# State-space input projections from seven quarter products, in four portions per chunk, with decays in place and five row buffers at the start

## Chip, core and metric

One core of one Trainium2 chip runs the whole program in one launch. The time is that of one execution on the device, in microseconds (us); a kernel's time is the median of several runs. The engines are named as in the profile: PE (TensorE) for matmuls, PEld for its weight loads, DVE (VectorE), ACT (ScalarE), POOL (GpSimd), and SP, whose queue issues most DMAs.

## Reference

All in float32, on 1024 tokens of width 512. Six steps are added to x one after another, each on the layer norm of x:

```
x = x + 0.5 * expert_ffn(norm(x))      # 8 experts, top 2, relu
x = x + attention(norm(x))             # 32 heads of 128, causal
x = x + 0.5 * expert_ffn(norm(x))
x = x + 0.5 * lora_ffn(norm(x))        # 512 x 512, plus a rank-8 expert of 4
x = x + state_space(norm(x))
x = x + 0.5 * lora_ffn(norm(x))
```

The change is mostly in the state-space step, with 64 heads of 64 channels in 8 groups and a state of 128:

```
proj = h @ in_proj_w.T                  # gate 4096 | x 4096, B 8x128, C 8x128 | dt 64
xBC  = silu(conv_bias + sum_k pad(x,B,C)[:, k:k+L] * conv_weight[:, k])    # 4 taps
dt   = softplus(dt + dt_bias);  dA = exp(dt * A)
state_t = state_{t-1} * dA_t + (dt_t * x_t) B_t ;  y_t = state_t . C_t + D * x_t
yn   = y * rsqrt(mean over the group of y^2 + eps) * norm_weight * silu(gate)
out  = yn @ out_proj_w.T
```

## The kernel before

The tokens are eight tiles of 128 (`NT`), x stays in SBUF in float32, and `hT` holds the normalized rows transposed: 128 partitions by four k-blocks (`KT`) by 1024 tokens. A list-scheduling layer (tiles with pools) takes the program order, places instructions on each engine's in-order queue, moves independent ones past each other, and adds the semaphore waits that tiles in use need. So the order on an engine is close to the text, but not equal to it.

**The start.** `expert_ffn` loads all expert weights, and `before_rows` runs `gate_steps` over the eight tiles: `normalize` writes the row `ln_xn` (pool `lnp`, two buffers, L169) and stores it to DRAM through ACT's queue (L172); then come the transposes into `hT` and the gate's logits. After the routing, rows are gathered back by indirect DMA on POOL's queue.

**Attention** already forms its projections from seven products of quarters: `sums` (L621) makes sums of weight quarters on POOL (L632), `products` (L246) the seven products, `mm_qk` (L821) and `mm_v` (L794) issue the matmuls, the latter with 256 columns (L797).

**State space** (`mamba`, L905). A first pipeline of tiles finishes the second expert step, runs the lora step, and computes dt, its decays and their running products; `decay` in DRAM holds the decays and their cumulative products in a form that can be broadcast to all partitions. Then come the units: `units` lists 8 groups times 2 halves of the tokens. A unit has four chunks of 128 tokens. While the scan of one unit runs, the projections of the next are interleaved:

- `project_pair(un, j)` (L1092): j = 0 for B and C, 1 and 2 for x, 3 and 4 for the gate. It fills one PSUM tile `ps_in` of 128 x 1024 (pool `pbig`, two buffers) by `project` (L227): two outputs, each four matmuls of 512 columns. A float32 matmul is two records in the profile. `plan` puts j = 0 and 1 beside chunk 0, then one pair beside each of chunks 1, 2 and 3.
- `conv_silu` (L1053): ACT writes the current tap with the bias (L1055), DVE adds three taps (L1059), reading `ps_in` in PSUM; in the second half, three more short steps take the last three columns of the first half from `hist` (L1068), which the first half keeps (L1077); ACT applies silu (L1078). D x is one ACT step per 128 channels over the half (`xd`, L1122).
- `finish_bc` (L1129): transposes of B and the products of B and C, masked into `gt`.
- `prepare(un, i)` (L1151): loads a chunk's decays twice over (`dd`, L1157, SP's queue), makes the segment decays `e_seg` by a DVE scan (L1163) and a product with `gt` (L1171), `xdt` = dt x from transposes (L1176), `xw` on POOL (L1182) and `cs` on POOL (L1188).
- `scan(un, i)` (L1196): `ps_y` (L1206), `y_m` (L1215), its squares (L1219) that POOL folds (L1238, L1239), `yg` (L1221), and the state: `ps_st` (L1224), POOL's decay of the state (L1231) and DVE's addition (L1234).
- `project_out` (L1243): the sum of squares `ps_ss` (L1247), its power on DVE and POOL (L149, L150), the output `ps_out` (L1258) and its addition to x (L1261).

`load_group(g)` issues the four weight loads of a group (`w_bc`, `w_x`, `w_g`, `w_out`) before its first projection; `wpool` has four buffers, so each waits for the last reader of the same weights of the group before. The loop's body is:

```
done = scan(un, i, *ready)
for j in plan[i]:
    project_pair(nxt, j)
if i == 1: finish_bc(nxt)
ready = prepare(un, i + 1)        # or prepare(nxt, 0)
project_out(*done)
```

Of the kernel before, what the change touches and what calls it, by code (L numbers as in the profile page):

```python
# [75 lines left out]
def macaron_kernel(  # L76
# [82 lines left out]
    def normalize(t, keep=False, pin=False):  # L159

        st = lnp.tile([P, 6], F32, tag="st", name="ln_st")
        nc.vector.bn_stats(st, x[:, t, :])
        mv = lnp.tile([P, 2], F32, tag="mv", name="ln_mv")
        nc.vector.bn_aggr(mv, st)
        rs = lnp.tile([P, 1], F32, tag="rs", name="ln_rs")
        root = rsqrt(rs, mv[:, 1:2], 1.0, EPS, 1)
        if pin:
            tc.keep_in_program_order(root)
        xn = lnp.tile([P, D], F32, tag="xn", name="ln_xn")  # L169
        nc.vector.tensor_scalar(xn, x[:, t, :], mv[:, 0:1], rs, ALU.subtract, ALU.mult)  # L170
        if keep:
            nc.scalar.dma_start(rows[t * P : (t + 1) * P, :], xn)  # L172
        normal[t] = xn
# [108 lines left out]
    def gates(t):  # L282
# [3 lines left out]
    gate_steps = (  # L286
        lambda t: normalize(t, True),
        transpose_h,
        None,
        lambda t: narrow_by_columns(t, gate_w, NE),  # L290
        gates,
    )
# [328 lines left out]
    def sums(pool, a11, a12, a21, a22, name, later=None):  # L621

        n = a11.shape[-1]
        ss = pool.tile([P, 3, 2, n], F32, tag=name, name=name)
        s1, s2, s4 = (ss[:, i, :, :] for i in range(3))
# [239 lines left out]
    class Scan:  # L865


        def __init__(self, pool):
# [9 lines left out]
            self.av = tile([P, MH], "av")  # L878

# [25 lines left out]
    def mamba(lora, par):  # L905
        conv, dsk, nwt, w_dt, dtb, av = par.conv, par.dsk, par.nwt, par.w_dt, par.dtb, par.av
        nct = MI // P
        with ExitStack() as ms:
# [10 lines left out]

            bcp = ms.enter_context(tc.tile_pool(name="m_bc", bufs=2))  # L920
            bp = ms.enter_context(tc.tile_pool(name="m_b", bufs=1))
            with tc.tile_pool(name="m_dt", bufs=1) as dp, tc.tile_pool(
# [5 lines left out]
                def pair():  # L928
                    return pairp.tile([P, 2, D], F32, tag="pair", name="pair")

# [70 lines left out]
                def add_bias(t):  # L1001
# [4 lines left out]
                    if t % nh == nh - 1:  # L1006
                        steps_of_time(t // nh)
# [15 lines left out]
            w2 = ms.enter_context(tc.tile_pool(name="m_w2", bufs=2))  # L1023
            ep = ms.enter_context(tc.tile_pool(name="m_e", bufs=2))
# [5 lines left out]
            def load_group(g):  # L1030

                gr = {"g": g, "state": None}
# [7 lines left out]
                gr["w_x"] = weights(in_wt[:, MI + g * 512 : MI + (g + 1) * 512], "w_x")  # L1040
                gr["w_g"] = weights(in_wt[:, g * 512 : (g + 1) * 512], "w_g")
# [8 lines left out]
                gr["hist"] = bcp.tile([P, 6, 3], F32, tag="hist", name="hist")  # L1050
                return gr

            def conv_silu(ps, ct, dst, hist, first):  # L1053

                nc.scalar.activation(  # L1055
                    dst, ps, AF.Identity, bias=conv[:, ct, 4:5], scale=conv[:, ct, 3:4]
                )
                for s in (1, 2, 3):
                    nc.vector.scalar_tensor_tensor(  # L1059
                        dst[:, s:],  # L1060
                        ps[:, : half - s],
                        conv[:, ct, 3 - s : 4 - s],
                        dst[:, s:],
# [3 lines left out]
                    if not first:  # L1067
                        nc.vector.scalar_tensor_tensor(  # L1068
                            dst[:, :s],
                            hist[:, 3 - s :],  # L1070
                            conv[:, ct, 3 - s : 4 - s],
                            dst[:, :s],
                            ALU.mult,
                            ALU.add,
                        )
                if first:
                    nc.vector.tensor_copy(hist, ps[:, half - 3 :])  # L1077
                nc.scalar.activation(dst, dst, AF.Silu)  # L1078

            def begin_unit(gr, hf):  # L1080
# [7 lines left out]
                un["xd"] = bcp.tile([P, 4, half], F32, tag="xd", name="xd")  # L1088
# [3 lines left out]
            def project_pair(un, j):  # L1092

                gr, g, hf = un["gr"], un["g"], un["hf"]
                ps = pbig.tile([P, S], F32, tag="pb", name="ps_in")
                w, col = ((gr["w_bc"], 0), (gr["w_x"], 0), (gr["w_x"], 256),
                          (gr["w_g"], 0), (gr["w_g"], 256))[j]
                for i in range(2):
                    project(ps, i * half, w, col + i * P, half, hf * half)
                if j > 2:  # L1100
                    i = 2 * (j - 3)
                    nc.scalar.activation(
                        un["sg"][:, i : i + 2, :].rearrange("p i c -> p (i c)"), ps, AF.Silu
                    )
                    return
                for i in range(2):
                    if j == 0:
                        dst = (un["bT"], un["cT"])[i]
                        ct = nct + i * MG + g
                    else:  # L1110
                        dst = un["xc"][:, 2 * (j - 1) + i, :]
                        ct = 4 * g + 2 * (j - 1) + i
                    conv_silu(
                        ps[:, i * half : (i + 1) * half],
                        ct,
                        dst,
                        gr["hist"][:, 2 * j + i, :],
                        hf == 0,
                    )
                    if j > 0:  # L1120
                        k = 2 * (j - 1) + i
                        nc.scalar.activation(  # L1122
                            un["xd"][:, k, :],
                            un["xc"][:, k, :],
                            AF.Copy,
                            scale=dsk[:, 4 * g + k : 4 * g + k + 1],
                        )
# [23 lines left out]
            def prepare(un, i):  # L1151
# [3 lines left out]
                dd = ep.tile([P, 2, HPG * P], F32, tag="dd", name="dd")  # L1155
                for q in range(2):
                    nc.sync.dma_start(  # L1157
                        dd[:, q, :],
# [3 lines left out]
                e = ep.tile([P, HPG, P], F32, tag="e", name="e_seg")  # L1162
                nc.vector.tensor_tensor_scan(  # L1163
                    e.rearrange("p h l -> p (h l)"),
                    dd[:, 0, :],
# [9 lines left out]
                xdt = w2.tile([P, D], F32, tag="xdt", name="xdt")  # L1175
                nc.vector.tensor_tensor(  # L1176
                    as_heads(xdt), as_heads(ps), per_head(dtp, un, i), ALU.mult
                )
                xw = None
                if c < NCH - 1:  # L1180
                    xw = w2.tile([P, D], F32, tag="xw", name="xw")
# [4 lines left out]
                if c > 0:  # L1186
                    cs = ep.tile([P, HPG, P], F32, tag="cs", name="cs")
# [3 lines left out]
                        dd[:, 1, :].rearrange("p (h l) -> p h l", l=P),  # L1191
                        ALU.mult,
                    )
                return e, xdt, xw, cs

            def scan(un, i, e, xdt, xw, cs):  # L1196
# [6 lines left out]
                for n, (left, right) in enumerate(terms):  # L1203
# [10 lines left out]
                y = w2.tile([P, 4, P], F32, tag="y", name="y_m")  # L1214
                nc.vector.tensor_tensor(  # L1215
                    y, py.rearrange("p (k l) -> p k l", l=P), un["xd"][:, :, tok], ALU.add
                )
                sq = w2.tile([P, 4, P], F32, tag="sq", name="sq")
                nc.scalar.activation(sq, y, AF.Square)  # L1219
                yg = w2.tile([P, 4, P], F32, tag="yg", name="yg")  # L1220
# [46 lines left out]
            gr = load_group(0)  # L1267
            un = begin_unit(gr, 0)
            for j in range(5):
                project_pair(un, j)  # L1270
                if j == 1:
                    finish_bc(un)
            ready = prepare(un, 0)
            plan = ((0, 1), (2,), (3,), (4,))
            for n, _ in enumerate(units):
                nxt = None
                if n + 1 < len(units):
                    g, hf = units[n + 1]
                    if hf == 0:
                        gr = load_group(g)  # L1280
                    nxt = begin_unit(gr, hf)
                for i in range(4):
                    done = scan(un, i, *ready)
                    if nxt is not None:
                        for j in plan[i]:
# [85 lines left out]
```

## Time and profile before

| | |
|---|---|
| median of 3 runs | 3006.68 us (3005.69 to 3007.23) |
| profiled execution | 3000.76 us, span 2999.0 us |
| mean granted clock of PE | 0.982 |
| busy PE, PEld | 2834.1 us (94%), 1525.5 us (51%) |
| busy DVE, ACT, POOL | 1691.8 us (56%), 711.6 us (24%), 782.8 us (26%) |
| DMA | 196.94 MB, mean 66 GB/s |

Busy time is the union of an engine's instructions; their records overlap a little at the ends, by some 0.08 us on DVE, so spacing is shorter than duration. The span can be cut into stages: the first expert step up to about 150 us, attention up to about 1640, the second expert step up to about 1800, the lora step and the decays up to about 1900, then the units up to about 2930. The shares of the whole span mix these stages, so each part of the change is read in its own. A line in a row is the line of the kernel before; "idle before" is the time for which the engine stood just before that group, with what ended it.

### The profile page before, as it was taken

How to read it: one execution, taken by the hardware profiler on the slowest of the kernel's cores; microseconds unless marked ns; L12 is line 12 of the kernel's file. 1: busy time of each engine (PE TensorE's matmuls, PEld its weight loads, DVE VectorE, ACT ScalarE, POOL GpSimd, SP SyncE). 2: the span in 40 equal slices, each digit the busy share in tenths (PEclk: the TensorE clock that was granted, in tenths of full speed). 3: DMA queues.
4: the chain of work that ended last, by engine and by line, in shares of the span. 5: the costliest groups of instructions: out<-in, count | busy, mean ns of one | idle time of the engine just before them, and what ended most of it. 6: DMA issues, size and time to landing. Idle time of an engine off the chain costs nothing.

```text
span 2999.0 us, 29327 instructions
## 1 busy us (share of the span) xinstructions
PE 2834.1 (94%) x10715; PEld 1525.5 (51%) x10715; DVE 1691.8 (56%) x3183; ACT 711.6 (24%) x1381; POOL 782.8 (26%) x593
## 2 busy tenths in 40 slices
PE   5979999999999999999999797899999999999989
PEld 3435646456464565645655343455555555555554
DVE  3145546465453654546545315677776777767673
ACT  1212212122121221213212121522222232322220
POOL 3231002020020200202000123144545545555450
PEclk8989999999999999999999898999999999999999
DMA  8420001010010100101002542232232322323210
GB/s 284 127 74 29 14 15 31 12 43 15 15 43 1 43 15 14 43 5 38 15 15 64 187 122 57 84 99 78 99 105 84 120 78 99 103 85 108 99 43 29
DMA packets 102174, 196.94 MB, mean 66 GB/s; under 512 B 9040, under 2 KB 34800, under 8 KB 102032
## 3 DMA queue, kind: packets, MB, share of 16 engines
q1 hardware_dynamic: 84896, 157.15, 15.7%
q0 software_dynamic: 6240, 20.45, 2.8%
q10 hardware_dynamic: 10896, 17.47, 1.5%
q8 instruction: 87, 1.43, 0.2%
q14 instruction: 55, 0.45, 0.1%
HBM read 176.17 MB, written 18.87 MB: 65 GB/s over the span
## 4 chain that ended last, share of the span: by engine, by line
PE 78%; DVE 12%; POOL 4%; issue 3%; DMA 2%; ACT 0%; POOLq 0%; DVEq 0%; SPq 0%; ACTq 0%
PE ps_in L227 14%; PE ps_m L823 13%; PE ps_o L728 8%; PE ps_wo L763 7%; PE ps_tr L156 6%; PE ps_m L797 6%; PE ps_out L1258 6%; PE ps_e L506 5%; PE ps_s L704 4%; DVE nm L715 3%; PE ps_y L1206 3%; PE ps_up L238 2%; DVE pr L720 1%; PE ps_st L1224 1%; DVE xc L1059 1%
## 5 line engine op out<-in xcount | busy, mean ns | idle before, releaser
L704 PE MATMUL ps_s<-kT,qT 128*128 128x512 f32 (+3 forms) x768 | 293.1, 491 | 1.8
L749 ACT COPY pT<-ps_tr 128x256 f32<-128x256 f32 (+2 forms) x192 | 91.9, 479 | 820.0 <-PE ps_tr L156 817.5
L728 PE MATMUL ps_o<-pT,v 128*128 128x512 f32 (+3 forms) x768 | 259.4, 488 | 0.0
L1258 PE MATMUL ps_out<-w_out,yg 128*128 128x512 f32 x512 | 240.4, 614 | 3.1 <-DVE yg L1221 3.1
L227 PE MATMUL ps_in<-hT,w_g 128*128 128x512 f32 x512 | 227.1, 596 | 7.9 <-issue 7.9
L227 PE MATMUL ps_in<-hT,w_x 128*128 128x512 f32 x512 | 225.8, 593 | 0.0
L1188 POOL TENSOR_TENSOR cs<-cT,dd 128x1024 f32<-128x1024 f32 x56 | 182.3, 3255 | 162.6 <-PE ps_y L1206 138.8
L763 PE MATMUL ps_wo<-w_o,oT 128*128 128x512 f32 x512 | 222.1, 593 | 0.0
L718 ACT ACTIVATE pr<-ps_s,nm 128x128 f32<-128x128 f32 (+7 forms) x256 | 190.3, 743 | 132.4 <-DVE nm L715 107.7
L728 PEld LDWEIGHTS ps_o<-pT,v 128*128 128x128 f32 x768 | 146.2, 191 | 142.6 <-issue 106.1
L156 PE MATMUL ps_tr<-ident,pr 128*128 128x128 f32 x1152 | 173.0, 277 | 31.1 <-DVE sm L719 22.9
L632 POOL TENSOR_TENSOR sv<-w_v 128x512 f32<-128x512 f32 x7 | 8.9, 1270 | 724.1 <-DMA w_v<-in_wkv_dram 607.3
L156 PEld LDWEIGHTS ps_tr<-ident,pr 128*128 128x128 f32 x1152 | 134.6, 142 | 115.1 <-issue 51.8
L715 DVE TENSOR_REDUCE nm<-ps_s 128x1 f32<-128x128 f32 (+7 forms) x256 | 189.2, 750 | 2.2
L506 PE MATMUL ps_e<-w_all,xt_s 128*128 (+1 forms) x368 | 167.0, 598 | 0.0
L227 PEld LDWEIGHTS ps_in<-hT,w_g 128*128 128x128 f32 x512 | 96.8, 191 | 127.5 <-issue 127.5
L227 PEld LDWEIGHTS ps_in<-hT,w_x 128*128 128x128 f32 x512 | 97.1, 190 | 120.8 <-issue 120.5
L1163 DVE TENSOR_TENSOR_SCAN e_seg<-dd,eye 128x1024 f32<-128x1024 f32 x64 | 154.2, 2409 | 6.9 <-PE ps_y L1206 5.7
L704 PEld LDWEIGHTS ps_s<-kT,qT 128*128 128x128 f32 x768 | 128.1, 193 | 54.7 <-issue 33.7
L763 PEld LDWEIGHTS ps_wo<-w_o,oT 128*128 128x128 f32 x512 | 96.4, 190 | 115.6 <-issue 115.6
L1059 DVE SCALAR_TENSOR_TENSOR xc<-ps_in,conv,xc 128x511 f32<-128x511 f32 (+2 forms) x192 | 141.6, 737 | 18.0 <-ACT xc L1055 17.6
L720 DVE TENSOR_SCALAR pr<-pr,sm 128x128 f32<-128x128 f32 (+7 forms) x256 | 145.4, 568 | 4.5
(252 smaller groups left out, 4401.8 us busy)
## 6 DMA issues: line engine op xcount, KB each, us to landing
dd<-decay SPq DMA_DIRECT2D x128, 512.0 KB, 4.5
w_all<-in_w_e_dram SPq DMA_DIRECT2D x16, 1024.0 KB, 10.3
outs<-y_e ACTq DMA_DIRECT2D x46, 256.0 KB, 3.6
w_v<-in_wkv_dram SPq DMA_DIRECT2D x8, 1024.0 KB, 5.2
w_q<-in_wq_dram SPq DMA_DIRECT2D x32, 256.0 KB, 4.3
w_k<-in_wkv_dram SPq DMA_DIRECT2D x8, 1024.0 KB, 5.2
w_o<-in_wo_dram SPq DMA_DIRECT2D x8, 1024.0 KB, 5.1
w_x<-in_in_wt_dram SPq DMA_DIRECT2D x8, 1024.0 KB, 7.8
```

The source lines that it names most:

```text
L156: nc.tensor.transpose(ps[:, i * P : (i + 1) * P], src(i), ident)
L227: nc.tensor.matmul(ps[:, cols : cols + n], lhsT=w[:, k, c0 : c0 + P], rhs=hT[:, k, t0 : t0 + n], start=(k == 0), stop=(k == KT - 1),)
L506: nc.tensor.matmul(ps, lhsT=xt[:, k, :], rhs=w_all[:, bass.ds(ep, 1), k, :].rearrange("p e c -> p (e c)"), start=(k == 0), stop=(k == KT - 1),
L704: nc.tensor.matmul(ps[:, j : j + m], lhsT=qT[:, qt * P : (qt + 1) * P], rhs=kT[:, j : j + m], start=True, stop=True,)
L715: nc.vector.tensor_reduce(nm, ps[:, :n], AX.X, ALU.max, negate=True)
L718: nc.scalar.activation(pr[:, :n], ps[:, :n], AF.Exp, bias=nm, accum_out=sm)
L728: nc.tensor.matmul(ps[:, lo:512], lhsT=v[:, kb, hh * P : (hh + 1) * P], rhs=pT[:, kb, lo:512], start=(kb == 0), stop=(kb == last),)
L763: nc.tensor.matmul(ps, lhsT=heads[hh][:, t * P : (t + 1) * P], rhs=w[:, hh, :], start=(hh == 0), stop=(hh == HG - 1),)
L797: nc.tensor.matmul(ps[:, t * 256 : (t + 1) * 256], lhsT=right[i][:, k, (j + t) * P : (j + t + 1) * P], rhs=left_v[i][:, k, :], start=(firs ...
L823: nc.tensor.matmul(ps, lhsT=gr["left"][i][:, k, hh * P : (hh + 1) * P], rhs=right[i][:, k, :], start=(first and k == 0), stop=(last and k ...
L1188: nc.gpsimd.tensor_tensor(cs, un["cT"][:, tok].unsqueeze(1).to_broadcast([P, HPG, P]), dd[:, 1, :].rearrange("p (h l) -> p h l", l=P), ALU ...
L1258: nc.tensor.matmul(po, lhsT=yg[:, k, :], rhs=w_o[:, k, :], start=(k == 0), stop=(k == 3))
```

## The change

**Seven products.** For each half, `quarter` makes the sums of the four quarters of `hT` once (on DVE, two k-blocks by 256 tokens each), one of them in place. `sums` makes those of the weights for B and C together, for x and for the gate, on POOL, into fixed tiles or into the free half of `w_bc`. A pair is now seven products of two matmuls with 256 columns in one PSUM tile: `pa` in one bank, `pb` and `pc` in the other. Three snapshots of `pa` go to SBUF by ACT, DVE adds them to `pb` and `pc`.

**Four portions.** `project_pair` is a generator; its four portions are placed before the scan, after it, after `prepare` and after `project_out`. The results of x, B and C go to `raw` tiles in SBUF with three columns ahead of them (zeros or `hist`), and the convolution reads those, one chunk later (`early`).

**Decays in place.** `e_seg` and `cs` overwrite the loaded `dd`. D x is made by chunks in `prepare`. Several buffers go from two to one.

**Weight loads** are issued over the chunks of the unit before, in place of all at once.

**First rows.** The first pass of `gate_steps` writes its rows to a pool `own` of five buffers.

```diff
-    def normalize(t, keep=False, pin=False):
+    def normalize(t, keep=False, pin=False, own=None):
...
-        xn = lnp.tile([P, D], F32, tag="xn", name="ln_xn")
+        if own is None:
+            xn = lnp.tile([P, D], F32, tag="xn", name="ln_xn")
+        else:
+            xn = own.tile([P, D], F32, tag="own", name="xn_own")
...
+                def quarter(hf):
+                    q1, q2 = (slice(hf * 512 + i * 256, hf * 512 + (i + 1) * 256) for i in range(2))
+                    b11, b12 = hT[:, :2, q1], hT[:, :2, q2]
+                    b21, b22 = hT[:, 2:, q1], hT[:, 2:, q2]
+                    t1, t2, t4 = (tt[:, hf, i, :, :] for i in range(3))
+                    nc.vector.tensor_tensor(t1, b12, b11, ALU.subtract)
+                    nc.vector.tensor_tensor(t2, b22, t1, ALU.subtract)
+                    nc.vector.tensor_tensor(t4, b21, t2, ALU.subtract)
+                    nc.vector.tensor_tensor(b12, b22, b12, ALU.subtract)
+                    quarters.append({1: b11, 2: b21, 3: b22, 4: t4, 5: t1, 6: t2, 7: b12})
...
             def conv_silu(raw, ct, dst):
                 nc.scalar.activation(
-                    dst, ps, AF.Identity, bias=conv[:, ct, 4:5], scale=conv[:, ct, 3:4]
+                    dst, raw[:, 3:], AF.Identity, bias=conv[:, ct, 4:5], scale=conv[:, ct, 3:4],
                 )
                 for s in (1, 2, 3):
                     nc.vector.scalar_tensor_tensor(
-                        dst[:, s:],
-                        ps[:, : half - s],
+                        dst,
+                        raw[:, 3 - s : 3 - s + half],
                         conv[:, ct, 3 - s : 4 - s],
-                        dst[:, s:],
+                        dst,
...
+                def mm(dst, i, first=False):
+                    for k in range(2):
+                        nc.tensor.matmul(dst, lhsT=left[i][:, k, c0 : c0 + P],
+                                         rhs=quarters[hf][i][:, k, :], ...)
+                snap = sn.tile([P, 3, n], F32, tag="snap", name="snap")
+                mm(pa, 1, True)
+                nc.scalar.copy(snap[:, 0, :], pa)
+                mm(pb, 2, True)
+                yield
+                mm(pa, 6)
+                nc.scalar.copy(snap[:, 1, :], pa)
+                mm(pc, 5)
+                yield
...
+                mm(pa, 7)
+                nc.scalar.copy(snap[:, 2, :], pa)
+                nc.vector.tensor_tensor(d1[:, :n], pb, snap[:, 0, :], ALU.add)
+                nc.vector.tensor_tensor(d2[:, n:], pc, snap[:, 2, :], ALU.add)
+                yield
+                mm(pc, 3)
+                nc.vector.tensor_tensor(d1[:, n:], pc, snap[:, 1, :], ALU.add)
+                mm(pa, 4)
+                if gate:
+                    nc.scalar.activation(d2[:, n:], d2[:, n:], AF.Silu)
+                    nc.scalar.activation(d2[:, :n], pa, AF.Silu)
+                    nc.scalar.activation(d1, d1, AF.Silu)
                     return
+                nc.scalar.copy(d2[:, :n], pa)
...
-                e = ep.tile([P, HPG, P], F32, tag="e", name="e_seg")
+                e = dd[:, 0, :, :]
...
-                    cs = ep.tile([P, HPG, P], F32, tag="cs", name="cs")
+                    cs = dd[:, 1, :, :]
...
+                    go_on(pairs)
                     done = scan(un, i, *ready)
+                    go_on(pairs)
+                    for f in early:
+                        f()
+                    if nxt is not None and i == 2:
+                        finish_bc(nxt)
                     if i < 3:
                         ready = prepare(un, i + 1)
                     elif nxt is not None:
                         ready = prepare(nxt, 0)
+                    go_on(pairs)
                     project_out(*done)
+                    go_on(pairs)
+                    if more and nxt["hf"] == 1:
+                        if i == 0:
+                            ahead = begin_group(nxt["g"] + 1)
+                            load_bc(ahead)
+                        elif i == 1:
+                            load_x(ahead)
+                            left_bc(ahead)
+                        elif i == 2:
+                            left_in(ahead, "x")
+                        else:
+                            load_g(ahead)
+                    elif nxt is not None and nxt["hf"] == 0:
+                        if i == 0:
+                            left_in(gr, "g")
+                        elif i == 3:
+                            load_o(gr)
...
-        expert_ffn("f0", Tiles(*gate_steps).flush, later)
+        def gates_of_input():
+            with tc.tile_pool(name="own", bufs=5) as own:
+                Tiles(*gate_steps(own)).flush()
+        expert_ffn("f0", gates_of_input, later)
```

## The prediction

> **What bounds the kernel now.** I read the page first (busy shares), then busy time by stage, then one unit of the state-space stage instruction by instruction, and last the rows of what the change adds.
>
> Two neighbouring units of the state-space stage, from the table by stretches (us, then busy time of PE, PEld, DVE, ACT and POOL, granted clock, DMA share, GB/s):
>
> ```profile
> 2331.00:2394.00 63.00, 62.38 (x281) 32.30 (x280) 47.94 (x67) 16.61 (x25) 33.37 (x23) 1.00 0.31 99
> 2394.00:2458.00 64.00, 64.00 (x272) 32.86 (x271) 44.49 (x59) 17.13 (x26) 31.88 (x23) 1.00 0.27 94
> ```
>
> A unit (one group, half the tokens, four chunks) takes 63.6 us and PE is busy for practically all of it at full clock. DVE works 46 us, POOL 33. So PE bounds this stage, and PE work that goes away is time won, as long as PE never starts to wait.
>
> The products, from the timeline of PE; the first row is a pair of projections now (eight matmuls of 512 columns, two records each), the others are quarter products of 256 columns in the attention stage:
>
> ```profile
> 2235.08 7.03 PE L227 MATMUL ps_in<-hT,w_g 128*128 128x512 f32 x16
> ...
> 312.31 1.89 PE L797 MATMUL ps_m<-w_v,hT 128*128 128x256 f32 x8
> 314.04 1.89 PE L797 MATMUL ps_m<-sv,tt 128*128 128x256 f32 x8
> ```
>
> Eight records of 256 columns start 1.73 us apart, 0.216 each, with new weights for every one; those of 512 columns come 0.43 apart (6.86 us per pair).
>
> VectorE and GpSimd in one place of the same stage:
>
> ```profile
> 1908.84 2.35 POOL L1188 TENSOR_TENSOR cs<-cT,dd 128x1024 f32<-128x1024 f32 x1 [21.69 <-DMA dd<-decay]
> 1909.17 4.16 DVE L1163 TENSOR_TENSOR_SCAN e_seg<-dd,eye 128x1024 f32<-128x1024 f32 x1
> 1913.23 2.34 POOL L1188 TENSOR_TENSOR cs<-cT,dd 128x1024 f32<-128x1024 f32 x1 [2.04 <-DMA dd<-decay]
> ```
>
> The scan takes 2.28 us elsewhere; here 4.16, and it ends 2.3 after the first cs ended; the second cs starts when the scan ends. They exclude each other. Whole-kernel rows say the same (min, median and max in ns):
>
> ```profile
> L1171 DVE TENSOR_TENSOR e_seg<-e_seg,gt x64: 1207/1572/2740, 1932.5 to 2922.4; 128x1024 f32<-128x1024 f32 x64
> L1188 POOL TENSOR_TENSOR cs<-cT,dd x56: 2343/3526/4112, 1908.8 to 2920.5; 128x1024 f32<-128x1024 f32 x56
> L1215 DVE TENSOR_TENSOR y_m<-ps_y,xd x64: 658/678/692, 1944.1 to 2960.3; 128x512 f32<-128x512 f32 x64
> L1059 DVE SCALAR_TENSOR_TENSOR xc<-ps_in,conv,xc x192: 650/737/751, 1908.5 to 2871.3; 128x511 f32<-128x511 f32 x64, 128x510 f32<-128x510 f32 x64, 128x509 f32<-128x509 f32 x64
> L1068 DVE SCALAR_TENSOR_TENSOR xc<-hist,conv,xc x84: 201/206/1741, 2087.0 to 2872.0; 128x1 f32<-128x1 f32 x28, 128x2 f32<-128x2 f32 x28, 128x3 f32<-128x3 f32 x28
> ```
>
> Where both inputs lie in SBUF (e_seg, and even the three-column hist step) the duration stretches by a POOL operation; where one comes from PSUM (y_m, the convolution now) it does not.
>
> **Part 1, the products.** A pair becomes 7 products x 2 k x 2 records = 28 records of 256 columns: 28 x 0.2157 = 6.04 us against 6.86, 0.82 saved. Of 80 pairs, 75 run inside the loop: 62 us. The first five lie beside the DVE chain that ends the stage before (PE sat idle 7.9 us there at 1914), so I count nothing for them, plus or minus 8.
>
> **Part 2, what DVE and ACT get.** Per pair ACT copies three snapshots of 128x256 (0.37 each in the attention's pT copy, L749) and one part more for x, B and C: some 6 us more per unit on an engine that works 17. D x by chunks is 16 small activations for 4 large ones, below 1 us more. DVE adds three 128x256 sums per pair, one input in PSUM (0.42 by the line through 0.29 for 128 and 0.68 for 512 columns): 15 x 0.35 net of overlap, 5 us per unit; the hist steps and copies (2 us) go. Quarters of hT: eight steps of 0.67 once. DVE is then near 49 of 60 us, ACT 24: neither is full.
>
> **Part 3, the SBUF side that DVE and POOL share.** The convolution now reads its source from the raw tile in SBUF, not from PSUM: 18 steps of 0.69 per unit (between 0.42 for 256 and 1.23 for 1024 columns, L953 and L690) move to the side that POOL excludes. No row of 512 columns shows this form under contention; the row nearest to it is the hist step, same operation and same inputs' place, which does stretch. Bounds: no exclusion, or all of it; I take all. The sums of the weights (L632 on 128x512: 1.27 us) are twelve new POOL steps per group, eight of 1.27 and four of about 0.65: 12.8 us. For two units, at the shortest durations seen: POOL cs 7 x 2.34, xw 7 x 1.04, state 6 x 1.04, sq 8 x 1.17, ss 8 x 0.55 = 43.7, with the sums 56.5. DVE with two SBUF inputs: 8 x (2.28 + 1.21 + 0.68) = 33.4, hist 3.6, together 37; after, 33.4 + 36 x 0.69 = 58.2. The shared side carried 81 of 127.2 us; it will carry 115 of the 119 that PE would leave. That cannot be packed without waiting.
>
> The Trainium skill (SBUF — State Buffer, Who interferes with whom) states it as a rule: a DVE instruction with two SBUF inputs locks out a GpSimd instruction that reads SBUF for its whole length. By the rule the convolution loses its immunity fully; by the y_m row alone it would lose nothing and the sum would be that of the first rival.
>
> Who waits for that? In the built order the waits are by whole tile: the second product waits for the first snapshot though it fills another bank, the fifth for the second snapshot, the third for two DVE additions, the fourth for the last addition. PE is in order; behind the waiting matmul stand ps_y, the transposes and ps_out. Twelve convolution steps stand in chunk 1, six in chunk 2, ahead of the additions that PE awaits. Walk of chunk 1, from the last addition of chunk 0: eight convolution steps, spaced 0.62, end at 5.7; y_m waits for ps_y until 6.3. From there POOL has sq, state, sq, xw, cs and ss (6.2 us), DVE yg, four convolution steps, the scan and the product (6.6), and they exclude each other: 12.8 us, ending near 20, and x and the last addition (1.1) follow at 21 to 22. PE is ready for its fourth product at 17: 4 to 5 late. With no exclusion the same row ends at 17.0, exactly in time.
>
> Chunk by chunk, for a group's two units: chunk 1, 5 twice; the sums for B and C land in chunk 1, 2.5 (0 to 3); those for x in chunk 2, behind a load of 8 us and ahead of cs and ss, 5 (0 to 8); those for the gate in chunk 0, ahead of the sq steps that ps_out waits for, 4 (0 to 5); snapshots queued on ACT behind silu and sq steps that wait for DVE, 3 per unit (1 to 4). Sum 10 + 2.5 + 5 + 4 + 6 = 27.5; some of these waits overlap, I take 23 (9 to 31). Against it stand 10 pairs x 0.82 = 8.2. Net +14.8 per group, x 7.5 groups = +111 us (+6 to +171).
>
> Waits of over 3 us may also slow the clock: after the gap of 7.9 us a record of 512 columns took twice its time.
>
> ```profile
> 1911.79 2.74 PE L227 MATMUL ps_in<-hT,w_x 128*128 128x512 f32 x6
> 1922.42 2.05 PE L227 MATMUL ps_in<-hT,w_g 128*128 128x512 f32 x2 [7.89 <-issue]
> ```
>
> A gap of 2.4 us at 79 left it full. I put no term in for this, only 1.7 us per wait, two per unit at worst, 50 us, at the upper end. The skill (TensorE: Matmul & The Clock Gate, Part 1) has the clock fall after one idle window of about 3.4 us; by that figure two waits per group would cost an estimated 25 us.
>
> **Part 4, five row buffers.**
>
> ```profile
> DVE ln_xn L170 <- DMA rows<-ln_xn: 14.6, 5, 5.4
> ```
>
> In the first 35 us DVE waits five times, 14.6 us, for a row's store before it may write the next. With five buffers the third to fifth rows wait for nothing and the last three for stores issued early. The logits then end near 28 instead of 34.8; routing follows, but its gathers fall into the weight loads that run until about 50. I take -6 (0 to -10).
>
> **Decays in place.** dd is now held until ps_y has read it, so the load for a chunk starts a chunk (13 us) ahead; it lands in 4.5. Covered; if not, ps_y waits for the difference. The weight loads are spread over chunks on SP, behind dd loads that wait for ps_y; they cost only what the sums above cost.
>
> **Sum.** The profiled execution took 3000.76 (span 2999.0, 1.8 around it), 5.9 below the median of 3006.68. 3000.8 + 111 - 6 = 3105.8; as a median 3111.7, say 3112.
>
> **Rivals.** First, faster: the waits stay below 8.2 us per group because sums run in the 30 us where DVE has little to do and the convolution hardly meets POOL. For it: chunk 0 holds two pairs and so 6 us more of PE work to hide behind, and DVE itself is not full. Against: 115 of 119. Place: chunks 1 and 2; price 0.82 per pair; it decides at 9 us of waits per group. Time 3006.7 - 62 - 6 = 2939, up to 3000 with half the waits. Chance 0.21. Second: the shared side matters little and PE waits for snapshots on ACT, two per pair, at 1 us: 10 per unit less 4.1, x 15 = +88, less 6: 3089. For: ACT is in order and holds steps that wait for DVE. Against: ACT is busy for 40%. Chance 0.14. Third: no change, waits eat exactly the 68 us, or PE's quarter products cost what the old ones did: 3007 within 6, chance 0.04. The forecast has 0.61.
>
> **Numbers.** Differences within 0.2% (6 us) can't be told from none here. Slower 0.61 + 0.14 = 0.75, same 0.04, faster 0.21. Range 2985 to 3190: below it three quarters of the faster case (0.15), above it the full waits with the slow clock (0.04). The forecast's own range is 3010 to 3185.
>
> **What would show it.** Right: a unit of about 71 us; PE busy near 84% there and waiting for DVE additions in chunks 1 and 2; the convolution above 0.9 us on average with a maximum over 2; cs above 3.3; 0.216 per record of ps_in; the wait for row stores below 5 us. Wrong: units of 59 to 62 us with PE full (first rival); waits of the matmuls named for ACT with the convolution at 0.69 (second); records of ps_in 0.245 apart (third).

## The result, and the profile after

The changed kernel took 3196.06 us (median of 4 runs, 3195.21 to 3199.76), the kernel before 3006.39: ratio 1.0635, 95% interval 1.0621 to 1.0649. The profiled execution spans 3192.2 us against 2999.0, at a granted clock of 0.959 against 0.982. It is slower, as forecast, but by 190 us where 105 were forecast, 6 us above the upper end of the range.

Two neighbouring units, from the table by stretches (us, busy PE, PEld, DVE, ACT, POOL, clock, DMA share, GB/s):

```profile
2044.60:2121.00 76.40, 69.81 (x357) 48.70 (x358) 53.29 (x71) 30.37 (x73) 29.23 (x23) 0.93 0.23 76
2121.00:2198.50 77.50, 62.28 (x319) 42.74 (x315) 50.04 (x62) 22.63 (x57) 51.61 (x40) 0.96 0.25 82
```

A unit takes 77 us, not 63.6. PE is busy for 132 of 154 us, no other engine is anywhere near full, and the clock is no longer 1.00. What PE waits for, from the view of waits over the state-space units (us in total, times, longest); first the only line of the kernel before, over six groups, then the changed kernel's largest, over all units:

```profile
PE ps_ss L1247 <- POOL sq L1239: 3.7, 12, 0.4
```

```profile
PE ps_in L1167 <- DVE sg L1204: 65.7, 22, 6.7
PE ps_in L1167 <- DVE raw L1204: 37.3, 21, 3.5
PE ps_ss L1351 <- POOL sq L1343: 27.3, 16, 3.1
PE ps_ss L1351 <- DVE raw L1200: 12.3, 6, 2.5
```

Two thirds are the fourth product (`mm(pa, 4)`, the last of the seven to be issued) waiting for the last addition (L1204). For snapshots it waited 0.3 us in all. The longest of these waits, in the timeline:

```profile
2298.85 1.27 POOL L638 TENSOR_TENSOR s_x<-w_x 128x512 f32<-128x512 f32 x1
...
2299.69 2.57 DVE L1259 TENSOR_TENSOR_SCAN dd<-dd,eye 128x1024 f32<-128x1024 f32 x1
...
2300.20 3.13 POOL L638 TENSOR_TENSOR s_x<-s_x,w_x 128x512 f32<-128x512 f32 x1
...
2302.90 1.51 DVE L1267 TENSOR_TENSOR dd<-dd,gt 128x1024 f32<-128x1024 f32 x1
...
2303.29 2.24 POOL L638 TENSOR_TENSOR w_x<-w_x 128x512 f32<-128x512 f32 x1
...
2305.50 1.25 POOL L638 TENSOR_TENSOR s_x<-w_x,s_x 128x512 f32<-128x512 f32 x1
...
2306.76 1.03 POOL L1286 TENSOR_TENSOR xw<-xdt,erev 128x512 f32<-128x512 f32 x1
2307.76 2.33 POOL L1292 TENSOR_TENSOR dd<-cT,dd 128x1024 f32<-128x1024 f32 x1
2310.05 0.54 POOL L150 TENSOR_TENSOR ss<-ss,neg_half 128x1 f32<-128x1 f32 x1
2310.63 0.75 DVE L1365 SCALAR_TENSOR_TENSOR x<-ps_out,ss,x 128x512 f32<-128x512 f32 x1 [6.22 <-POOL ss L150]
2311.30 0.41 DVE L1204 TENSOR_TENSOR sg<-ps_in,snap 128x256 f32<-128x256 f32 x1
```

The chain reads from the top: four weight sums on POOL (two of them stretched by the scan and the product that DVE runs meanwhile), then xw, cs and ss; DVE's x waits for ss; the addition stands behind x; and PE's fourth product waits for the addition, which reads another bank of the same PSUM tile. What follows on PE:

```profile
2304.00 1.03 PE L1167 MATMUL ps_in<-hT,w_g 128*128 128x256 f32 x4
2311.77 2.08 PE L1167 MATMUL ps_in<-tt_m,w_g 128*128 128x256 f32 x4 [6.74 <-DVE sg L1204]
```

Four records that take 1.03 us at full clock take 2.08 after the gap: it is paid twice, as idle time and as slow work. The convolution from SBUF, and cs (min/median/max in ns):

```profile
L1132 DVE SCALAR_TENSOR_TENSOR xc<-raw,conv,xc x192: 718/751/2833, 1921.0 to 3074.0; 128x512 f32<-128x512 f32 x192
```

```profile
L1292 POOL TENSOR_TENSOR dd<-cT,dd x56: 2328/2844/4392, 1924.8 to 3126.1; 128x1024 f32<-128x1024 f32 x56
```

Now the sum. In both traces I took the stretch from the first ps_out matmul of the first chunk to that of the 61st, gave each PE record the time to the next one's start, less idle time, and split that by the granted clock:

| From chunk 1 to 61, us | before | after | difference | forecast |
|---|---|---|---|---|
| PE waits | 7.7 | 156.9 | +149 | +172 |
| PE work lost to a slow clock | 0 | 58.9 | +59 | 0 |
| products (ps_in), at full clock | 502.0 | 480.2 | -22 | -62 |
| ps_y, at full clock | 107.7 | 125.2 | +17 | 0 |
| other PE work, and rest | 331.6 | 329.0 | -3 | 0 |
| sum | 949.1 | 1150.2 | +201 | +111 |
| ahead of it | 1958.4 | 1953.4 | -5 | -6 |
| behind it | 91.5 | 88.6 | -3 | 0 |

### The profile page after: what moved, and what is told of

It reads as the page before. It is cut to its first block, busy times and chain, and to the rows that moved or that the text cites. A ratio compares the mean times of both kernels' runs of the same rounds, so it can differ in the third digit from the quotient of the medians.

```text
span 3192.2 us, 32124 instructions
## 1 busy us (share of the span) xinstructions
PE 2880.0 (90%) x11675; PEld 1733.1 (54%) x11675; DVE 1792.2 (56%) x3239; ACT 856.0 (27%) x2015; POOL 905.7 (28%) x737
## 4 chain that ended last, share of the span: by engine, by line
PE 62%; DVE 18%; POOL 8%; DMA 6%; issue 4%; ACT 1%; SPq 0%; POOLq 0%; ACTq 0%; DVEq 0%
PE ps_m L829 12%; PE ps_o L734 7%; PE ps_in L1167 7%; PE ps_wo L769 7%; PE ps_m L803 5%; PE ps_tr L156 5%; PE ps_e L510 4%; PE ps_s L710 4%; PE ps_y L1310 3%; DVE dd L1259 3%; DVE nm L721 3%; DMA dd<-decay 3%; DVE xc L1132 2%; PE ps_up L241 2%; PE ps_out L1362 2%
## 5 line engine op out<-in xcount | busy, mean ns | idle before, releaser
L1362 PE MATMUL ps_out<-w_out,yg 128*128 128x512 f32 x512 | 252.5, 636 | 0.0
L1259 DVE TENSOR_TENSOR_SCAN dd<-dd,eye 128x1024 f32<-128x1024 f32 x64 | 181.6, 2838 | 43.9 <-DMA dd<-decay 43.8
L1132 DVE SCALAR_TENSOR_TENSOR xc<-raw,conv,xc 128x512 f32<-128x512 f32 x192 | 173.5, 910 | 19.4 <-ACT xc L1124 18.3
L1292 POOL TENSOR_TENSOR dd<-cT,dd 128x1024 f32<-128x1024 f32 x56 | 157.2, 2807 | 22.5 <-DMA dd<-decay 15.3
L1362 PEld LDWEIGHTS ps_out<-w_out,yg 128*128 128x128 f32 x512 | 98.4, 203 | 97.8 <-issue 97.4
L1319 DVE TENSOR_TENSOR y_m<-ps_y,xd 128x512 f32<-128x512 f32 x64 | 44.1, 689 | 188.8 <-PE ps_y L1310 188.5
L661 POOL TENSOR_SCALAR w_q<-w_q 128x1024 f32<-128x1024 f32 x16 | 44.3, 2770 | 364.1 <-DMA w_q<-in_wq_dram 363.4
L741 DVE COPY oT<-ps_o 128x512 f32<-128x512 f32 x64 | 44.0, 687 | 183.0 <-PE ps_o L734 183.0
```

The source lines that it names most:

```text
L1132: nc.vector.scalar_tensor_tensor(dst, raw[:, 3 - s : 3 - s + half], conv[:, ct, 3 - s : 4 - s], dst, ALU.mult, ALU.add,)
L1259: nc.vector.tensor_tensor_scan(e.rearrange("p h l -> p (h l)"), e.rearrange("p h l -> p (h l)"), eye8.rearrange("p h l -> p (h l)"), 0.0, ...
L1362: nc.tensor.matmul(po, lhsT=yg[:, k, :], rhs=w_o[:, k, :], start=(k == 0), stop=(k == 3))
```

## The experiments

The theory of the prediction: DVE and POOL share a side of SBUF that the change fills, so additions come late and PE waits. Rivals: the lateness is one of order and of the common PSUM tile; GpSimd's weight sums; the clock; snapshots on ACT. Ratios are to the kernel before, with 95% intervals. "Per group" is two units, the mean over six groups.

**The first rows alone** (the kernel before with the five row buffers, and no other part of the change).

```diff
-        expert_ffn("f0", Tiles(*gate_steps).flush, later)
+        expert_ffn("f0", gates_of_input, later)    # own pool, bufs=5
...
```

> The kernel before with five row buffers in the first stage and nothing else. The prediction's term: 6 us less (0 to 10), 3000 us. In the changed kernel the first expert product starts at 51.6 us instead of 57.0 and the last one of that stage ends 5.7 earlier, but the last attention product is only 2.4 earlier; so a rival says that half of it is lost again on the way: 3004. A third says that the start is bound by the loads: 3006.

Measured 0.9981 (0.9972 to 0.999), 6 us less: the first reading (3000), and the term as forecast. The waits for row stores went from 14.6 us to:

```profile
DVE xn_own L173 <- DMA rows<-xn_own: 2.7, 2, 2.2
```

**Two PSUM tiles**, so that the fourth product does not wait for an addition that it doesn't need.

```diff
-                ps = pbig.tile([P, S], F32, tag="pb", name="ps_in")
-                pa, pb, pc = ps[:, :n], ps[:, 2 * n : 3 * n], ps[:, 3 * n :]
+                psa = big[-1].tile([P, 512], F32, tag="pa", name="ps_in")
+                psb = big[-1].tile([P, 512], F32, tag="pbc", name="ps_ib")
+                pa, pb, pc = psa[:, :n], psb[:, :n], psb[:, n:]
...
```

> The changed kernel with the pair's PSUM buffer as two tiles (the snapshots' quarter in one, the two others in the second), so that the last product no longer waits for the last addition, which it does not need. Theory of order and tile: the additions are late because they stand on VectorE behind the scan, the product with the mask and x, and 13.7 of the 20.9 us of waits per group are for an addition that only the common tile makes PE wait for. They go, with them some 5 to 6 us per group of slow clock and 2 of ps_y: 133 us per group, 3020 to 3060. Theory of the prediction (the SBUF side that VectorE and GpSimd share is full): the lateness stays and is waited for at the next product: at least half of the loss remains, 3110 to 3190.

Measured 1.024 (1.0224 to 1.0255), 3077.7 us: 118 of the 190 us are gone, between the two readings. A group fell from 154.1 to 139.3 us: waits 21.0 to 13.2, clock 7.7 to 4.8, ps_y back from 16.7 to 14.3, products 65.3 to 63.3. (With one tile the scheduler had put product records between those of ps_y.) What is left are other waits:

```profile
PE ps_ss L1352 <- DVE sg L1202: 24.5, 6, 4.4
PE ps_in L1168 <- ACT snap L1183: 14.5, 15, 1.9
PE ps_in L1168 <- ACT sg L1209: 13.4, 8, 1.8
PE ps_ss L1352 <- POOL raw L1196: 11.2, 6, 2.0
```

**Without the weight sums**, in one tile and in two.

```diff
-                gr["l_" + n] = sums(None, w[:, :2, :256], ..., into=[...])
+                gr["l_" + n] = {1: a11, 2: a12, 3: a12, 4: a22, 5: a21, 6: a22, 7: a21}
...                                            # and the same for "l_bc"
```

> The changed kernel with the weight sums of the state-space projections left out (the products read the plain quarters, so the projections are not the reference's): twelve GpSimd steps per group less, everything else as it was. The prediction's terms for the sums: 2.5 + 5 + 4 = 11.5 us of waits per group, with the slow clock that hangs on them some 4 more: 7.5 x 15 = 115 us, about 3080. If only the wait of 6.7 us behind the sums for x goes, with its clock: 7.5 x 9 = 68, 3130. If GpSimd, busy for 40%, does not matter: 3196.

Measured 1.0427 (1.0411 to 1.0443), 3137.9: some 60 less, the middle reading (3130). Waits fell by 6 us per group, not by 11.5: without the sums the additions are still late behind the scan and x, and PE still waits 13.4 of 15.1 us per group for L1204's counterpart:

```profile
PE ps_in L1151 <- DVE raw L1188: 50.2, 26, 3.5
PE ps_in L1151 <- DVE sg L1188: 34.5, 19, 3.1
```

> Both: two PSUM tiles, and no weight sums (projections not the reference's). The convolution still reads from SBUF. Theory of order and sums: practically no waits are left and the clock stays up; a group takes 127.1 less the saving of the products (3.5 to 8): 119 to 124 us, 2945 to 2985 in all. Theory of the full shared side: even without the sums it carries 102 of 119 us; waits of 5 to 10 us per group remain with some slow clock, 3020 to 3090.

Measured 1.0117 (1.0102 to 1.0133), 3041.8: the second reading. 10.1 us of waits per group remain with no weight sum in the loop. So the common tile and the sums are not the whole story; the largest of the rest is ps_ss behind a fold of the squares on POOL that a scan stretches from 0.46 to 2.43 us:

```profile
2382.96 2.79 DVE L1244 TENSOR_TENSOR_SCAN dd<-dd,eye 128x1024 f32<-128x1024 f32 x1
...
2383.56 2.43 POOL L1328 TENSOR_TENSOR sq<-sq 128x128 f32<-128x128 f32 x1
```

**Useless work in PE's waits**, to part the clock from the waits.

```diff
                 mm(pc, 3)
+                for f in range({(3, 1): 14, (2, 0): 6, (2, 1): 3, (4, 0): 3}.get((j, hf), 0)):
+                    nc.tensor.matmul(ps[:, n : 2 * n], ..., start=False, stop=True)   # unread columns
```

A first version was sized wrongly, twice over (an instruction is two records) and for the wrong pair:

> The changed kernel, in which TensorE does useless work while it waits: ahead of the fourth product, 26, 12, 6 or 6 products of 256 columns into columns of the same PSUM tile that nobody reads, in the four pairs of a group whose last addition came 6.7, 3.5, 1.8 and 1.9 us late (2.8 to 5.6 us of PE work for the long ones, 10.8 per group). The additions come no earlier by it. Theory of the clock: the slow clock after gaps of over 2 us costs 7.7 us of the 154 per group; with the two long gaps filled it costs 3 to 4, and the time falls by 4 x 7.5 = 30 us to about 3166 although PE has more to do. If only the waits count, nothing changes: 3196 (3190 to 3205). If the filler does not fit into the waits, up to 81 us more: 3277.

Measured 1.0887 (1.0869 to 1.0904), 3270.5, near the last reading: 21.6 us of filler per group and the longest wait untouched; it told the size and nothing on the clock. The second, whose edit is the one above:

> The filler again, sized by what the first such run showed: an instruction of 256 columns is two records (0.43 us), and the longest wait belongs to the first gate pair of the second half. So 14, 6, 3 and 3 instructions in the pairs that wait 6.7, 3.5, 1.8 and 1.9 us: 11.2 us of useless work per group in 13.9 us of waits. Theory of the clock: with these gaps filled only the two for ps_ss are left, and of 7.7 us per group of slow clock about 3 remain; the time falls by 4.5 x 7.5 = 34 us to about 3162 (3150 to 3175). If only the waits count: 3196 (3190 to 3205).

Measured 1.0532 (1.0515 to 1.0548), 3165.2: 31 us less with 11.2 us more PE work per group, near the clock's reading and far from the other. One group, in the table by stretches, where the changed kernel's had clocks of 0.93 and 0.96:

```profile
2105.10:2252.40 147.30, 137.22 (x726) 97.83 (x724) 105.30 (x132) 53.23 (x130) 78.86 (x63) 0.99 0.25 83
```

Over the six groups a group fell by 4.9 us: the waits by 11.0, in whose place came 10.2 us more of work in ps_in, and the slow clock by 3.9, from 7.7 to 3.8. The clock term is real and separate from the waits.

**Decays in place, and the convolution from SBUF, in the kernel before.** The second kernel holds the first one's edit too.

```diff
-                e = ep.tile([P, HPG, P], F32, tag="e", name="e_seg")
+                e = dd[:, 0, :, :]
-                    cs = ep.tile([P, HPG, P], F32, tag="cs", name="cs")
+                    cs = dd[:, 1, :, :]
```

> The kernel before with the decays in place alone (scan, product with the mask and cs write into the tile that the load filled). The prediction's term: covered, 0 (3000 to 3012). The run with the convolution from SBUF held this edit too and took 40 us more than the kernel before, with VectorE and GpSimd waiting 128 us for the loads of the decays; if these waits are what it paid, this kernel takes 3035 to 3050, and the convolution from SBUF costs next to nothing.

```diff
+                raw = rw.tile([P, half], F32, tag="raw", name="raw")
+                nc.scalar.copy(raw, ps)
...
-                        ps[:, : half - s],
+                        raw[:, : half - s],
```

> The kernel before, whose convolution reads a copy in SBUF that ScalarE makes, in place of PSUM; full products as before; decays in place, to make room. Nothing else. Theory of the shared side: the convolution, 0.74 us on average now, goes to 0.85 to 0.95 with a maximum over 2, and cs stays at 3.5 or gets longer; PE does not wait for VectorE in this kernel, so the time stays within 10 us: 2997 to 3017. If a convolution from SBUF is not disturbed, it stays at 0.70 to 0.75. If VectorE and GpSimd cannot carry it beside the products, PE waits and the time grows by 20 to 60.

Decays alone: 1.0018 (1.0008 to 1.0027), 5 us. The forecast of nothing was slightly too good: 1.2 us per group of ps_y waiting for DVE, whose scan waits for its load. With the convolution from SBUF as well: 1.0133 (1.0117 to 1.015), so the second edit costs 35 us without any change to the products, the third reading. First row: PSUM source; second, in the other kernel: SBUF source.

```profile
L1059 DVE SCALAR_TENSOR_TENSOR xc<-ps_in,conv,xc x192: 651/741/751, 1910.5 to 2885.4; 128x511 f32<-128x511 f32 x64, 128x510 f32<-128x510 f32 x64, 128x509 f32<-128x509 f32 x64
```

```profile
L1062 DVE SCALAR_TENSOR_TENSOR xc<-raw,conv,xc x192: 733/745/2830, 1916.5 to 2924.4; 128x511 f32<-128x511 f32 x64, 128x510 f32<-128x510 f32 x64, 128x509 f32<-128x509 f32 x64
```

The medians agree, the maximum is nearly fourfold: most steps meet no POOL operation, some wait one out. PE, which I had thought independent of DVE here, waits 6.0 us per group (2.5 with the decays alone):

```profile
PE ps_y L1209 <- DVE xdt L1179: 21.4, 8, 4.1
PE ps_out L1261 <- ACT btok L1136: 11.4, 7, 3.4
```

The 35 us need not be the price of the source alone. The edit also gives ACT a copy for every 128 channels, into a tile with one buffer, and these copies waited 124.5 us in all for the convolution to be done with it; the second line is a wait for ACT. No run parts the copy from the source.

**Other orders of the two-tile kernel.**

```diff
-                mm(pc, 3)
-                nc.vector.tensor_tensor(d1[:, n:], pc, snap[:, 1, :], ALU.add)
                 mm(pa, 4)
+                mm(pc, 3)
+                nc.vector.tensor_tensor(d1[:, n:], pc, snap[:, 1, :], ALU.add)
...
+                po = psml.tile(...)    # ps_out's four matmuls, from behind ps_ss
                 pss = psml.tile([P, 512], F32, tag="ps", name="ps_ss")
...
-                            nc.gpsimd.memset(r[:, :3], 0.0)
+                            nc.vector.memset(r[:, :3], 0.0)    # in conv_both
...                                            # and the order of the silus
```

> The kernel with two PSUM tiles per pair, and four moves that change no work: the fourth product ahead of the third; ps_out ahead of the row sums ps_ss (whose folded squares come late from GpSimd); of a gate pair the silu that frees the PSUM tile first; the first three columns of raw set when the convolution begins, on VectorE and ScalarE, and no longer by a GpSimd step that waits for an old buffer. Theory of order: of 13.2 us of waits per group that the two-tile kernel has, 6.5 for ps_ss and 2.4 for silu and copy go, and 3 of 4.8 us of slow clock: 139.3 - 12 = 127.4 us per group, 2988 (2970 to 3010). Theory of the full shared side: the lateness is only handed on, to the third product and ps_y; half remains: 3035 or more.

Measured 1.0115 (1.0099 to 1.0131), 3040.0: 38 less than in two tiles alone, but the second reading (3035 or more). The waits for ps_ss are gone; PE now waits here:

```profile
PE ps_tr L156 <- DVE y_m L1318: 44.3, 13, 5.5
PE ps_in L1168 <- ACT snap L1183: 19.4, 23, 1.8
```

ps_tr takes the PSUM buffer that y_m frees, and y_m stands behind the convolution. Two attempts on that kernel: the first two additions ahead of the scan, and the transposes and products of B and C behind ps_ss.

```diff
+                    go_on(pairs)                       # additions ahead: from behind prepare
                     ready = prepare(un, i + 1)
-                    go_on(pairs)
```

> The same, with the third stage of a pair (the seventh product and the first two additions) put ahead of the scan of the next chunk in the program. The additions no longer stand behind the scan and the product with the mask. If that takes the last waits of PE: 122 to 125 us per group, 2950 to 2975. If the scan now comes too late for the next ps_y: 127 to 132, 2985 to 3025.

```diff
-                    if nxt is not None and i == 2:     # B and C behind: to after project_out
-                        finish_bc(nxt)
```

> The reordered two-tile kernel, with the transposes and products of B and C moved from ahead of ps_tr to behind ps_ss. There the transposes of xc waited 7.0 us per group for y_m, which frees their PSUM buffer. Theory of order: that wait and its slow clock go (133.0 - 7 to 8.5 = 124.5 to 126 us per group against 127.1 before): 2976 to 2990, faster than the kernel before. If the wait only moves to the next allocation (the products of B and C, or ps_y, which then waits for x): 3020 to 3040.

Both became slower: 1.0261 (1.0246 to 1.0275) and 1.0238 (1.0224 to 1.0252), neither reading's mechanism. The waits for y_m went, and another came that neither expectation had; in the second:

```profile
PE ps_in L1168 <- ACT snap L1183: 86.2, 27, 7.3
```

Here it is the snapshot, queued on ACT behind a silu that waits for the convolution on DVE, and behind the squares of y_m. In the first it is the same pair of lines with 84.3 us. That is my second rival's mechanism, which the changed kernel itself does not show.

**Seven products for the gate alone.** x, B and C in full products, the convolution from PSUM, 4 weight sums per group and not 12; two tiles and the order above, dd in three buffers, B and C finished one chunk earlier, five row buffers.

```diff
+                if j < 3:
+                    yield
+                    ...
+                        project(ps, 0, w, col + i * P, half, hf * half)
+                        conv_silu(ps, ct, dst, gr["hist"][:, 2 * j + i, :], hf == 0)
+                    return
-                left = gr["l_" + ("bc", "x", "x", "g", "g")[j]]
+                left = gr["l_g"]
...
```

> Seven products for the two gate pairs of a unit alone, in two PSUM tiles and with the order of the reordered kernel; x, B and C are projected in full again and the convolution reads PSUM as before; the sums of the weights are 4 GpSimd steps per group, not 12; decays in place with three buffers, five row buffers. If the convolution from SBUF and the sums for x, B and C are what VectorE and GpSimd could not carry, hardly a wait is left: four pairs save 0.5 to 0.8 us each, 2 to 3 per group, with the row buffers' 6 us: 2975 to 2990. If the additions and snapshots of the gate pairs alone are late: waits of 3 or more per group, 3000 to 3030.

Measured 0.989 (0.9873 to 0.9906), 2973.3 us: 2 us below the first reading's range, and 1.1% faster than the kernel before. One group:

```profile
2075.40:2199.90 124.50, 123.02 (x601) 74.56 (x600) 97.48 (x137) 44.13 (x96) 65.45 (x48) 1.00 0.30 98
```

PE is full again at full clock, with 1.5 us of waits per group. The gate's four pairs save 2.05 us per group, ps_out 1.4 (its records come 0.429 apart and not 0.451), the row buffers their 6 us. So of the gain some 15 us are the gate's products and 10 the place of ps_out, which no run changed by itself. The convolution reads PSUM again, and its maximum is 751 ns, its median 742. Which of the parts left out here (the convolution's source, the eight sums, the additions and snapshots of x, B and C) had cost how much, this kernel does not say.

## Why the prediction was wrong in size

The sign, the bound and most places of the waits were right. The terms, in the order of their error:

**Clock (0 forecast, +59).** The step that failed: "I put no term in for this". I had allowed 50 us at the upper end (1.7 us per wait, two per unit) and left it out of the sum, on the strength of one gap of 2.4 us in the trace of before that left the clock full. Measured were 27 slow stretches in 15 units, at 2.2 us each: more than that worst case. The trace after has 40 gaps of over 0.7 us between 1940 and 3000 us. Of the 14 of 3.3 us and more, all are followed by a stretch at half clock, which lasts 3.4, 6.8 or 10.2 us; of 18 between 1.9 and 3.3, 12; of 8 shorter ones, none. I forecast 23 us of waits per group, in pieces of 2.5 to 5; at that size the clock belongs into the sum. The filler run shows the term by itself. The Trainium skill (TensorE: Matmul & The Clock Gate, Part 1) names an idle window of about 3.4 us; here 5 of 9 gaps between 1.9 and 2.5 were enough.

The trace goes far to show what decides. All its slow stretches start at whole multiples of 3.41 us from the first of them. Divided into such windows, the state-space units have 27 at full clock that a slow one follows, and in each of them PE stood still for 1.85 us or more; of the other windows only two have as much (1.92 and 1.95). Around the wait shown above (after the window: us, busy PE, PEld, DVE, ACT, POOL, clock, DMA share, GB/s):

```profile
2305.39:2308.80 3.41, 0.00 (x0) 0.00 (x0) 0.00 (x0) 0.00 (x0) 3.41 (x5) 1.00 0.00 0
2308.80:2312.21 3.41, 0.44 (x1) 0.45 (x2) 1.08 (x2) 0.47 (x1) 1.79 (x2) 0.50 0.00 0
```

So a gap of 2 us counts where it falls into one window, and one of 3.15 us passed where the border at 2189.3 divides it into 1.95 and 1.20.

**Products (-62 forecast, -22).** The term "28 x 0.2157 = 6.04": 0.216 is the smallest spacing, and five in six of the records reach it, but the mean at full clock is 0.233, 65.3 us per group where 68.8 were before. In the row that I took it from, eight records followed each other without a wait; here many pairs of instructions have one of their own. In two tiles the mean was 0.226, which gives 2 of the 5 us per group that are missing; what holds back the rest was not tested apart. Product records between those of ps_y also broke up its runs of 16 (+17, forecast nothing; gone in two tiles).

**Waits (+172 forecast, +149).** Place by place, per group: chunk 1, forecast 5 + 5, measured 3.5 + 0.9 (1.8 in three of six groups); sums for B and C, 2.5 and 2.1; sums for x, 5 and 6.7; sums for the gate, 4 and 3.1; snapshots, 6 and nothing. Additions of gate pairs, which I had not listed, took 2.6, small ones 2.1. That the total came within 2 us of the 23 is in part luck: chunk 1 and the snapshots, 16 in the forecast, gave 4.4. And where the three places named for the sums have 11.9 us, leaving the sums out took only 6 away in all.

The cause was only half right. The shared side is real: convolution steps of up to 2.83 us show it. But two thirds of the waits stood at the end of in-order queues with a common tile, which I had read from the built order and not priced by itself: separating the tile took 118 us away, and left the work on the shared side as it was. How much the two engines held each other up can be estimated from the traces, as the time that their steps took beyond the shortest ones of their kind: some 35 us per group before, 43 after, and 36 in two tiles without the sums, where PE waited 0.6, 20.9 and 9.8. So the sum of what they lose to each other does not set PE's waits by itself. No run has the changed kernel's order without the shared side, so its part in the lateness stays open. (A small misreading: the scan at 1909.17 ends 2.1 us after the first cs, not 2.3.)

**Signs to look for.** Right: PE busy 86% (84 forecast); convolution 0.91 us on average and over 2 at most; rows' wait under 5 us. Wrong: cs above 3.3 us; its median fell from 3.53 to 2.84, and other POOL steps waited out DVE in its place (ss, 0.79 us on average before, 1.45 after). Wrong, too: 0.216 per record. The unit of 71 us came out at 77, by the clock and the products.

**Rivals.** Faster (0.21): the waits were 20 us per group more than before, not below 9. Snapshots (0.14): not in this kernel, but next in line, as two experiments show. No change (0.04): one of its conditions, records 0.245 apart, came more than halfway true with 0.233.

## What to carry to other kernels

Where PE is the bound, price a new wait twice: its length, and the stretch at half clock that follows it; fill it or split it before anything else. In this scheduling layer a tile that holds several results makes each writer wait for the readers of all; give results with different readers their own tiles. A DVE operand moved from PSUM to SBUF can make its step wait out a POOL step, so try first the part of such a change that leaves the operands where they are: the gate's products alone were a gain, if one of some 15 us in 3006.

## What the hardware showed beyond that

A POOL step of 128x1 elements (ss, L150) takes 0.54 us undisturbed. In the changed kernel 24 of 64 were near that, and 19 took about 2.5. One of these started 1.9 us into a scan and ended 0.3 after it:

```profile
2366.84 4.08 DVE L1259 TENSOR_TENSOR_SCAN dd<-dd,eye 128x1024 f32<-128x1024 f32 x1
...
2368.73 2.53 POOL L150 TENSOR_TENSOR ss<-ss,neg_half 128x1 f32<-128x1 f32 x1
```

So the size of an operation says nothing of what the shared side may cost it. The border of the clock windows is less sharp in other kernels: in the two-tile kernel six of the 21 windows ahead of a slow one had 1.7 us of standstill or less, three of them 1.30 in short gaps between small matmuls. Why these were enough is left open.
